# Other steps for the weight factors and the sums of blocks in the first attention

## The chip, the core and the metric

The kernel runs on one core of a Trainium2 chip. The metric is the time of the whole launch on the device, in microseconds, here the median of three runs. A core has a matrix engine (TensorE, in the profile PE, its weight loads PEld), an engine for elementwise work and reductions (VectorE, DVE), one for activation functions (ScalarE, ACT), GpSimd (POOL) and SyncE (SP), which in this kernel issues nearly all DMAs.

## What is computed

Two attention blocks, one after the other, on 8 images of 512 channels and 32 x 32 pixels (1024 tokens), all in float32. Each block normalises in 8 groups of channels, makes q, k and v, attends with 8 heads of 64 channels, projects and adds its input:

```python
def block(x, gamma, beta, wq, wk, wv, bq, bk, bv, wp, bp):     # for one image, x: (512, 1024)
    xg = x.reshape(8, -1)
    xn = (xg - xg.mean(-1)) * rsqrt(xg.var(-1) + 1e-5)
    xn = xn.reshape(512, 1024) * gamma + beta
    q, k, v = wq @ xn + bq, wk @ xn + bk, wv @ xn + bv         # 8 heads of 64 rows
    attn = softmax(q.T @ k / 8)                                # for each head, 1024 x 1024
    out = (attn @ v.T).T
    return x + wp @ out + bp

x = block(x, L0...)
x = block(x, L1...)
```

The two layers have weights of their own; in the reference they come as one stacked qkv matrix for layer 0 and as three matrices for layer 1.

## The kernel before

There are 16 jobs, an image and a layer each, in the order (image 0, layer 0), (1, 0), (0, 1), (1, 1), then the next two images. For each job the kernel runs an attention, and between two attentions a stretch of projections: v of the next job, the output projection of this job, then k and q of the next job. The projections use Strassen's scheme with seven products instead of eight (v one level deep, the others two levels), so weights and inputs are needed as sums of their blocks. That gives VectorE three kinds of work that the change and the prediction name:

- weight factors: four sums for each weight matrix (`factor`, L151 to L160; S1, S2, S3, S4), made once for each layer and matrix, written to DRAM by `store_factors` (L162, DMAs of L168) and read back later as tiles w of a ring of seven;
- sums of blocks of the normed input xn (`combine`, L380 to L391, tile t), and the deep sums of these (`inner_sums`, L401 to L429, tile deep);
- sums of blocks of the attention's output (L534 to L539, and `combine` on tile to), in the stretch after an attention.

`Attention.run` (L984) writes the attention down step by step. There are 8 groups (pair of heads, half of the queries) of 8 steps, 64 steps in all, numbered i. In a step TensorE makes the scores of step i (L870, tile sc) and the products with v of step i - 2 (L901, tile po); ScalarE takes the exponential (L875, tile e, from a pool of six); VectorE adds e to the sum of its group (L885 for a group's second step, L887 afterwards, tile acc). At a group's last product `finish` (L906) follows: VectorE reduces acc (L917, tile r) and adds the two halves of po into q (L924), which frees po's banks. Every second group a gather of r (L944) goes out by SP, later VectorE inverts the sums (`invert`, L948 to L968), SP spreads the inverses (rd, then rb, L961 and L963), and VectorE normalises q (L978). These follow at due times that the kernel's own count of microseconds sets (`later`, `advance`).

Other work is put into the steps as chores, one in a step. A taken step sends a chore on to the next free one:

```python
def put(i, fn):
    while i in chores:
        i += 1
    chores[i] = fn
```

In the attention of job n, chores prepare job n + 1. Only in the first attention (n = 0) are there, besides the weight factors of output layer 0 and v layer 1, also the statistics of the next image's norm. `norm_steps(1)` gives as its reads: four sums and four squares on ScalarE (L244, L252), between them `less_mean` (L249), and at the end `by_count` (L258, on VectorE, tile mv) with `gather` (L271): SP writes mv to DRAM as dm, in two DMAs (L275), and reads it back as gm (L279) when dm has landed. Its steps are `groups` (L286 to L291: VectorE on gm, then a power on GpSimd, then SP writes dg and reads it back as mr, L293 and L296), `factors` (L304 to L306, from mr) and four times `apply` (L311, xn on ScalarE). The factors of weights are put first, then the reads, then the steps with the sums of blocks, and the last four deep sums. The slot of each chore in the first attention, as `put` gives it out:

| chore | before | after |
|---|---|---|
| blocks of weights sent for | 2 | 2 |
| factors of output, layer 0; store | 12, 15, 18, 21; 22 | 8, 10, 12, 14; 15 |
| factors of v, layer 1; store | 24, 27, 30, 33; 34 | 16, 18, 20, 22; 23 |
| sums of the norm; less_mean | 4, 5, 6, 7; 8 | 4, 5, 6, 7; 9 |
| squares of the norm | 10, 11, 13, 14 | 11, 13, 17, 19 |
| by_count and gather | 16 | 21 |
| groups; factors of the norm | 23; 31 | 24; 30 |
| apply | 35, 36, 37, 38 | 34, 35, 36, 37 |
| sums of blocks | 41, 44, 47, 50 | 39, 41, 43, 45 |
| deep sums | 52, 54, 57, 59 | 47, 49, 51, 53 |

The order on TensorE, ScalarE and VectorE is the order in which the program is written, so a chore stands in VectorE's queue between two sums of e. SP's order follows from the program and from when its inputs are expected: in the first attention it is dm, dm, gm, r, store, rd, rb, rb, store, dg, mr before, and store, store, r, store, rd, dm, rb, rb, dm, store, gm, dg, mr after.

After the attention the banks of both halves of PSUM are given out anew (`banks`), and v's first products on the right half need po's last banks, which L924 frees.

Of the kernel before, what the change touches and what calls it, by code (L numbers as in the profile page):

```python
# [40 lines left out]
K, V, Q, O = range(4)  # L41
# [31 lines left out]
def fast_path(  # L73
# [34 lines left out]
    def later(delay, fn):  # L108
        todo.append((clock[0] + delay, fn))
# [36 lines left out]
    def load_blocks(w, layer, which):  # L146
        for i in range(2):
            for j in range(2):
                nc.sync.dma_start(w[:, 2 * j + i], raw_block(layer, which, i, j))

    def factor(w, part):  # L151

        if part == 0:
            nc.vector.tensor_add(w[:, S1], w[:, S3], w[:, A22])
        elif part == 1:
            nc.vector.tensor_sub(w[:, S2], w[:, S1], w[:, A11])  # L156
        elif part == 2:
            nc.vector.tensor_sub(w[:, S3], w[:, A11], w[:, S3])
        else:
            nc.vector.tensor_sub(w[:, S4], w[:, A12], w[:, S2])  # L160

    def store_factors(w, layer, which):  # L162
        keep = wdram.tile([P, NW, 2, CH], F32, name=f"keep_{which}_{layer}")
        if (which, layer) == (O, 1):
            nc.sync.dma_start(keep, w)
        else:
            for s in (slice(S1, NW), slice(S3, S3 + 1)):
                nc.sync.dma_start(keep[:, s], w[:, s])  # L168
        factors[which, layer] = keep
# [3 lines left out]
    def fetch():  # L173


        if not plan or len(held) == RING:
            return
        key = plan.popleft()
        n, which, o = key
        layer = jobs[n][1]  # L180
        w = ring.tile([P, NW, P], F32, tag="w", name=f"w_{which}_{n}_{o}")
        held[key] = w
        if (which, layer, o) in deep:
            nc.sync.dma_start(w, deep[which, layer, o])
        else:
            if o in BLOCK:
                src = raw_block(layer, which, *BLOCK[o])
            else:
                src = factors[which, layer][:, FACTOR[o]]
            nc.sync.dma_start(wide(w), src)  # L190
            if which != V:
                raw.add(key)
# [20 lines left out]
    def x_tile(b):  # L213
        xs[b] = xpool.tile([P, NC, S], F32, tag="x", name=f"x_{b}")
        return xs[b]

    def load_x(b):
        for cc in range(NC):
            nc.sync.dma_start(xs[b][:, cc, :], x[b, cc * P : (cc + 1) * P, :])

    class Norm:
# [20 lines left out]
        def sums(self, cc):  # L242

            nc.scalar.activation(  # L244
                xn[0][:, cc, :], xs[self.b][:, cc, :], AF.Identity, accum_out=self.mv[:, cc, 0:1]
            )
# [523 lines left out]
    def last_weights(n):  # L770
        w = acts.tile([P, NW, 2, CH], F32, tag="deep", name="w_last")
        nc.sync.dma_start(w, factors[O, jobs[n][1]])
        return w
# [10 lines left out]
    def last_sums(sh):  # L784


        def start():
            if sh == 0:
                tx[0] = acts.tile([P, 3, 2, HALF], F32, tag="t", name="t_last")
            nc.vector.tensor_sub(last_right(sh, 5), last_right(sh, 7), last_right(sh, 1))  # L790

        def second():
            nc.vector.tensor_sub(last_right(sh, 6), last_right(sh, 3), last_right(sh, 5))

        def third():
            nc.vector.tensor_sub(last_right(sh, 7), last_right(sh, 3), last_right(sh, 7))

        def fourth():
            nc.vector.tensor_sub(last_right(sh, 4), last_right(sh, 2), last_right(sh, 6))

        return start, second, third, fourth
# [241 lines left out]
    def deep_steps(n):  # L1043


        made = []

        def sums_(part, direct):
            if not made:
                made.append(True)  # L1050
                d = acts.tile([P, 4, 7, QT], F32, tag="deep", name=f"deep_{n}")
                deep_x[0], deep_t[0] = d[:, :, :4, :], d[:, :, 4:, :]
            inner_sums(part, direct)

        return [
            lambda part=part, direct=direct: sums_(part, direct)
            for direct in (True, False) for part in range(4)
        ]

    def extend_plan(n):  # L1060
        plan.extend((n, V, o) for o in ORDER)
        plan.extend((n - 1, O, o) for o in ORDER)
        plan.extend((n, which, o) for which in (K, Q) for o in OUTER)
# [29 lines left out]

        return load, [lambda oc=oc: add_up(oc) for oc in range(NC)]

    def first_factors(put, which_layers):

        box = []

        def start():  # L1100
            box.append(acts.tile([P, 2, NW, 2, CH], F32, tag="deep", name=f"raw_{len(factors)}"))
            for i, (which, layer) in enumerate(which_layers):
                load_blocks(box[0][:, i], layer, which)

        put(2, start)
        at = 9
        for i, (which, layer) in enumerate(which_layers):
            for part in range(4):
                at += 3
                put(at, lambda i=i, part=part: factor(box[0][:, i], part))  # L1110
            put(at + 1, lambda i=i, which=which, layer=layer: store_factors(
                box[0][:, i], layer, which
            ))
# [162 lines left out]
    for n in range(-1, len(jobs)):  # L1276
        last = n + 1 == len(jobs)
        outs = None
        if n >= 0:
            chores = {}  # L1280
# [6 lines that stand above are left out]
            if last:  # L1287
                w = last_weights(n)
                for i, fn in enumerate(last_sums(0)):
                    put(44 + 3 * i, fn)  # L1290
            else:
                if n == 0:
                    first_factors(put, [(O, 0), (V, 1)])
                elif n == 1:
                    first_factors(put, [(K, 1), (Q, 1)])
                elif n == 2:
                    first_factors(put, [(O, 1)])
                for i, (_, fn) in enumerate(extra):
                    put(2 + i, fn)
                at = (10, 19, 22, 24, 26, 28, 36, 39, 42, 45)  # L1300
                if n == 0:
                    for i, fn in zip((3, 3, 4, 5, 6, 8, 10, 11, 12, 13, 15), reads):
                        put(i, fn)
                    at = (22, 30, 34, 35, 37, 38, 41, 44, 47, 50)
                for i, fn in zip(at, steps + sums(n + 1)):
                    put(i, fn)
                deep_first = deep_steps(n + 1)
                for at, fn in zip((52, 54, 57, 59), deep_first[4:]):
                    put(at, fn)
                put(61, lambda: (extend_plan(n + 1), [fetch() for _ in range(RING)]))  # L1310
            assert max(chores, default=0) < NT * len(att.groups)
            att.run(chores)
            banks(0, "one")
            banks(1, "one")
            if last:
                for i, fn in enumerate(last_sums(1)):
                    later(7.0 + 0.8 * i, fn)
                later(13.0, judge)
                for sh in range(2):
                    last_proj(n, w, sh)  # L1320
                break
            outs = OutputSums(n)
            out_sums(n, outs)
            first = v_phase(n + 1, ORDER)
            for thunk in first[:-1]:
                thunk()
            rest = first[-1:]
            extra = deque()
            if jobs[n][1] == 1 and jobs[n][0] + 2 < B:
                extra.append((11, lambda b=jobs[n][0] + 2: (x_tile(b), load_x(b))))  # L1330
            if n == 1:
                load, bias_steps = make_out_bias(1)
                extra.append((8, load))
                extra.extend((11, fn) for fn in bias_steps)
            if n + 2 < len(jobs):
                reads, steps = norm_steps(n + 2)
                extra.extend((15, fn) for fn in reads)
        both = deep_phases(n + 1, extra, outs, deep_first[:4] if outs else ())
        both[0]()
        rest[0]()  # L1340
        if n < 0:
            later(22.0, lambda: load_x(1))
        for thunk in both[1:]:
            thunk()
        banks(0, "two")
        att = Attention(n + 1)
        att.scores(0)
        att.scores(1)
        banks(1, "two")
        att.scores(2, "po")  # L1350
# [249 lines left out]
```

## Time and profile before

| | us |
|---|---|
| median of three runs (lowest, highest) | 3205.2 (3205.03, 3205.63) |
| the profiled execution: time, span | 3206.06, 3204.3 |
| TensorE, VectorE, ScalarE busy | 3185.3, 2772.8, 1914.4 |
| first attention, TensorE from first scores to last product | 81.57 to 191.7 |
| stretch to the second attention | 191.7 to 287.13 |
| second attention; stretch to the third | 287.13 to 397.16; to 489.78 |

An attention takes 110 us, of which a step is 1.72; the stretch after the first attention takes 95.4 us, the one after the second 92.6. The span is what lies between the first and the last instruction; the execution's own time is 1.76 us longer. TensorE ran at its full clock throughout.

How it is to be read: in a timeline a line gives start and duration of an instruction (or of several alike, with xcount), its engine, its line in the kernel, what it writes and reads, and in brackets the time that the engine was idle before it and what ended that. In the chain of waits every piece is the one that the next had to wait for. An engine that is busy is not thereby the bound: what counts is whether TensorE waits for it.

### The profile page before, as it was taken

Reading aid. Unit: us, or ns where it says so; the run is one execution under the profiler, and the core shown is the slowest. Engines: PE = TensorE matmul, PEld = TensorE weight load, DVE = VectorE, ACT = ScalarE, POOL = GpSimd, SP = SyncE. Lnnn points to the kernel's source line nnn. Section 1 sums busy time; section 2 is a strip of 40 time slices with the busy share of each in tenths; the row PEclk is TensorE's granted clock in tenths of the full one; section 3 lists DMA queues with packets and bytes.
Section 4 is the critical chain, followed back from the end, with each engine's and each line's share of the span. In section 5 each row is a group of like instructions: output and inputs, shape, how many; then the busy total and the mean of one; then the engine's idle time right before and its main releaser. Section 6 shows DMA issues by size and latency. Waiting matters only on the chain.

```text
span 3204.3 us, 57789 instructions
## 1 busy us (share of the span) xinstructions
PE 3185.3 (99%) x22917; PEld 1862.8 (58%) x22917; DVE 2772.8 (87%) x3989; ACT 1914.4 (60%) x3063; POOL 100.7 (3%) x95
## 2 busy tenths in 40 slices
PE   9999999999999999999999999999999999999999
PEld 7366384563836638366483754837547375573744
DVE  8897999979889798897988879888898888978878
ACT  4746646466565665656656565565656656566564
POOL 0000000000000000000000000000000000000000
PEclk9999999999999999999999999999999999999999
DMA  8234172350613305034170421504316051150611
GB/s 291 74 107 127 48 213 70 92 169 22 210 28 88 91 26 159 22 100 132 33 211 16 114 72 33 152 16 135 103 44 194 16 137 48 49 136 16 174 37 42
DMA packets 156998, 308.32 MB, mean 96 GB/s; under 512 B 34104, under 2 KB 60592, under 8 KB 156464
## 3 DMA queue, kind: packets, MB, share of 16 engines
q1 hardware_dynamic: 139856, 272.05, 26.8%
q0 software_dynamic: 16864, 32.51, 6.2%
q8 instruction: 181, 2.97, 0.4%
q14 instruction: 97, 0.79, 0.1%
HBM read 225.13 MB, written 45.68 MB: 85 GB/s over the span
## 4 chain that ended last, share of the span: by engine, by line
PE 95%; DVE 3%; DMA 1%; issue 0%; POOL 0%; ACT 0%; DVEq 0%; ACTq 0%; POOLq 0%
PE sc L870 28%; PE po L901 27%; PE zd L636 10%; PE vd L636 10%; PE z L494 6%; PE yd L636 5%; PE ud L636 4%; PE v L494 2%; PE y L494 2%; PE u L494 1%; PE z_last L814 0%; DMA x<-p 0%; DVE w L156 0%; DMA w<-deep 0%; DVE p L655 0%; DVE v L520 0%
## 5 line engine op out<-in xcount | busy, mean ns | idle before, releaser
L875 ACT ACTIVATE e<-sc 128x1024 f32<-128x1024 f32 x1024 | 1045.3, 1025 | 563.4 <-PE sc L870 457.4
L870 PE MATMUL sc<-q,k 64*64 64x512 f32 x8192 | 1058.0, 589 | 0.0
L901 PE MATMUL po<-e,v 64*64 64x512 f32 x8192 | 1057.1, 589 | 0.0
L887 DVE TENSOR_TENSOR acc<-acc,e 128x1024 f32<-128x1024 f32 x768 | 936.0, 1219 | 58.8 <-ACT e L875 12.1
L901 PEld LDWEIGHTS po<-e,v 64*64 64x64 f32 x8192 | 312.9, 133 | 566.0 <-issue 554.4
L870 PEld LDWEIGHTS sc<-q,k 64*64 64x64 f32 x8192 | 311.2, 133 | 562.7 <-issue 545.0
L885 DVE TENSOR_TENSOR acc<-e,e 128x1024 f32<-128x1024 f32 x128 | 156.3, 1221 | 112.3 <-ACT e L875 112.2
L636 PE MATMUL zd<-deep,w 128*128 128x256 f32 x860 | 241.1, 380 | 3.8 <-DVE p L653 1.7
L636 PE MATMUL vd<-deep,w 128*128 128x256 f32 x804 | 224.3, 380 | 2.1 <-DVE p L655 1.3
L636 PEld LDWEIGHTS zd<-deep,w 128*128 128x128 f32 x860 | 162.8, 190 | 28.2 <-DVE p L653 3.0
L636 PEld LDWEIGHTS vd<-deep,w 128*128 128x128 f32 x804 | 152.3, 190 | 24.6 <-DVE p L655 2.5
L917 DVE TRANSPOSE_TENSOR_REDUCE r<-acc 128x32 f32<-128x1024 f32 x128 | 158.5, 1238 | 0.6
L682 POOL DMA_DIRECT2D x<-p x62 | 74.6, 1211 | 1972.7 <-ACT p L646 1525.2
L636 PE MATMUL vd<-os,w 128*128 128x256 f32 x420 | 118.1, 380 | 1.6 <-DVE p L655 1.5
L668 DVE TENSOR_TENSOR p<-p,p 128x1024 f32<-128x1024 f32 x94 | 114.2, 1214 | 0.0
L494 PE MATMUL z<-w,t 128*128 128x256 f32 x480 | 110.9, 379 | 0.0
L494 PE MATMUL z<-w,xn 128*128 128x256 f32 x480 | 110.1, 382 | 0.0
L518 ACT COPY v<-z 128x512 f32<-128x512 f32 x32 | 18.8, 586 | 148.7 <-PE z L494 148.7
L494 PEld LDWEIGHTS z<-w,xn 128*128 128x128 f32 x480 | 90.0, 190 | 23.8 <-issue 12.2
L442 ACT COPY ud<-zd 128x256 f32<-128x256 f32 x156 | 55.7, 357 | 76.6 <-PE zd L636 75.1
L653 DVE TENSOR_TENSOR p<-vd,s 128x256 f32<-128x256 f32 x63 | 26.7, 424 | 85.6 <-PE vd L636 85.6
L657 ACT COPY s<-vd 128x256 f32<-128x256 f32 x156 | 58.1, 373 | 69.2 <-PE vd L636 69.2
(242 smaller groups left out, 4194.9 us busy)
## 6 DMA issues: line engine op xcount, KB each, us to landing
w<-deep SPq DMA_DIRECT2D x287, 448.0 KB, 3.8
x<-p POOLq DMA_DIRECT2D x62, 512.0 KB, 6.9
rb<-rd SPq DMA_DIRECT2D x96, 256.0 KB, 4.0
w<-keep SPq DMA_DIRECT2D x84, 256.0 KB, 2.7
deep<-w SPq DMA_DIRECT2D x42, 448.0 KB, 3.8
w<-wqkv_dram SPq DMA_DIRECT2D x57, 256.0 KB, 2.8
x<-x_dram SPq DMA_DIRECT2D x28, 512.0 KB, 6.4
out_dram<-x SPq DMA_DIRECT2D x28, 512.0 KB, 6.2
```

Source lines behind the costliest of these rows:

```text
L442: nc.scalar.copy(u, z)
L494: nc.tensor.matmul(ps[:, ti * CH : (ti + 1) * CH], right(src, tx[0], o)[:, cc, t0 : t0 + P], w[:, cc, :], start=(start and ti == 0 and cc ...
L636: nc.tensor.matmul(ps, lhs[:, FACTOR[i], :], moving[i], start=start, stop=True, skip_group_check=True,)
L657: return chain(product, lambda ps: nc.scalar.copy(s5, ps), put, z, y, u, w)
L668: outer.append(lambda: nc.vector.tensor_add(to_, a, b))
L682: nc.gpsimd.dma_start(to_, p(part), accum_op=ALU.add)
L870: nc.tensor.matmul(sc[h * HD : (h + 1) * HD, j, :], k[r, hp, k0 : k0 + HD], q[r, hp, sh * HALF : (sh + 1) * HALF], start=True, stop=True,)
L875: nc.scalar.activation(e, sc, AF.Exp, scale=SCALE)
L885: nc.vector.tensor_add(acc[g], self.es[i - 1], e)
L887: nc.vector.tensor_add(acc[g], acc[g], e)
L901: nc.tensor.matmul(po[g][j * HD : (j + 1) * HD, h, :], v[r, kc, d0 : d0 + HD], e[r, j, :], start=(kc == 0), stop=(kc == NT - 1),)
L917: nc.vector.tensor_reduce(self.r[:, 0, m, :], self.acc.pop(g).rearrange("p j (b e) -> p (j b) e", e=RP), AX.X, ALU.add, apply_transpose=True,)
```

## The change

In the first attention the weight factors start at step 8 and stand in every second step, where they started at step 12 and stood in every third. The sums of blocks are put from step 39 in every second step, and the last four deep sums follow in every second step from 47. Nothing else of the program is edited; chores whose step is now taken move, as the table above shows. The same instructions run on TensorE, VectorE and ScalarE.

```diff
-    def first_factors(put, which_layers):
+    def first_factors(put, which_layers, at=9, apart=3):
 
         box = []
...
         put(2, start)
-        at = 9
         for i, (which, layer) in enumerate(which_layers):
             for part in range(4):
-                at += 3
+                at += apart
                 put(at, lambda i=i, part=part: factor(box[0][:, i], part))
             put(at + 1, lambda i=i, which=which, layer=layer: store_factors(
                 box[0][:, i], layer, which
             ))
...
                 if n == 0:
-                    first_factors(put, [(O, 0), (V, 1)])
+                    first_factors(put, [(O, 0), (V, 1)], 6, 2)
                 elif n == 1:
                     first_factors(put, [(K, 1), (Q, 1)])
...
                 if n == 0:
                     for i, fn in zip((3, 3, 4, 5, 6, 8, 10, 11, 12, 13, 15), reads):
                         put(i, fn)
-                    at = (22, 30, 34, 35, 37, 38, 41, 44, 47, 50)
+                    at = (22, 30, 34, 35, 36, 37, 39, 41, 43, 45)
                 for i, fn in zip(at, steps + sums(n + 1)):
                     put(i, fn)
                 deep_first = deep_steps(n + 1)
-                for at, fn in zip((52, 54, 57, 59), deep_first[4:]):
+                for at, fn in zip((47, 49, 51, 53) if n == 0 else (52, 54, 57, 59), deep_first[4:]):
                     put(at, fn)
```

## The prediction

> **What bounds the kernel now.** I read four views, each to find where the one before it ends: the chain of waits (what the end hangs on), the waits of TensorE (how much could be won at all), the timeline around the first attention (who is late there), and the DMA queue of SP (what the moved steps send for). The page's line for the chain of waits first:
>
> ```profile
> PE 95%; DVE 3%; DMA 1%; issue 0%; POOL 0%; ACT 0%; DVEq 0%; ACTq 0%; POOLq 0%
> ```
>
> TensorE is the bound; the other engines count only where TensorE waits for them. Its waits between 80 and 290 us, the stretch that the change can touch (columns: us in total, times, longest):
>
> ```profile
> PE zd L636 <- DVE p L653: 1.7, 2, 1.1
> PE v L494 <- DVE q L924: 1.7, 1, 1.7
> PE zd L636 <- ACT yd L438: 1.6, 1, 1.6
> PE vd L636 <- DVE p L655: 0.6, 1, 0.6
> ```
>
> Together 5.6 us. This is the ceiling of any gain: 5.6 of 3205.2 us is 0.17%. I call 0.2%, 6.4 us, the least that a measurement of this kernel tells from no change.
>
> The timeline shows why the 1.7 us wait is there. These are VectorE's instructions that matter, and TensorE's late one:
>
> ```profile
> 111.18 1.23 DVE L885 TENSOR_TENSOR acc<-e,e 128x1024 f32<-128x1024 f32 x1 [0.81 <-ACT e L875]
> 120.85 0.60 DVE L948 TENSOR_REDUCE lt<-r 32x64 f32<-32x256 f32 x1 [2.51 <-DMA r<-r]
> 126.71 0.21 DVE L286 BATCH_NORM_STATS2 gs<-gm 8x6 f32<-8x64 f32 x1
> 196.87 1.25 DVE L917 TRANSPOSE_TENSOR_REDUCE r<-acc 128x32 f32<-128x1024 f32 x1
> 198.03 0.65 DVE L924 TENSOR_TENSOR q<-po,px 128x512 f32<-128x512 f32 x1
> 198.74 1.99 PE L494 MATMUL v<-w,t 128*128 128x256 f32 x8 [1.67 <-DVE q L924]
> ```
>
> The bracket is the engine's idle time. VectorE idles 8.0 us in the first attention (0.40, 0.73, 0.72, 1.56, 0.26, 0.20, 0.82, 0.81 and 2.51), all before 120.85. After that it shows no bracket until 235: it is late and works off a queue. TensorE has done the attention at 191.7, VectorE at 198.7. From 194.3 to 230.05 the chain of waits is VectorE's, then TensorE's. So the quantity to follow is VectorE's idle time in the first attention: **its work is not changed in amount, so the end of its queue moves by the change in idle time, and TensorE with it.**
>
> The DMA queue of SP in that stretch:
>
> ```profile
> 110.43 1.36 SPq L275 DMA_DIRECT2D dm<-mv  x2
> 116.76 0.38 SPq L279 DMA_DIRECT2D gm<-dm  x1
> 117.24 2.28 SPq L944 DMA_DIRECT2D r<-r  x3
> 122.38 0.34 SPq L961 DMA_DIRECT2D rd<-rt  x1
> 124.94 1.30 SPq L963 DMA_DIRECT2D rb<-rd  x2
> 126.34 0.54 SPq L168 DMA_DIRECT2D keep<-raw  x1
> ```
>
> The gather of the norm (dm to DRAM, then gm back) starts at 110.43, right after VectorE scales mv (L258, 110.20). Gm is sent for at 116.76, after SP waited 4.9 us for dm. VectorE uses it at 126.71, unhindered. And r, which VectorE lacks at 118.3, was sent for only at 117.24 because it stood behind gm.
>
> [...] 9.95 us lie between gm's issue and its use, and gm waits 4.9 us for dm. [...] The trace: 3.8 us to landing for dm (2 KB, to DRAM), 1.7 for r (8 KB, within SBUF). [...]
>
> **The change part by part.**
>
> (1) *Eight weight factors* (L154 to L160, 0.68 us each, 0.60 from start to start), from steps 12 to 33 to steps 8 to 22. Before 112.3 us VectorE now runs five of them instead of two: 3 x 0.60 = 1.8 us more in time that it idled. Its idle there falls from 5.5 to 3.7 us. The blocks of weights that they read are sent for at 81.6 to 86.5 and land within 7.5 us, by 94; the first factor now stands at 95.8. Nothing is waited for. Gain 1.8 us. Stores of factors go to SP earlier, ahead of r; they wait for factors that are done by 108.4.
>
> (2) *What the factors push aside.* A step holds one chore; a taken step sends the chore to the next free one. The table of steps is filled with factors first, so the statistics of the next image move: the last square from step 14 to 19, and L258 with the gather from step 16 to 21. The first use of gm, groups (L286), was put at 22 and moves only from 23 to 24. **The distance between sending and using falls from 7 steps to 3, of 1.72 us each.** This is the cost of the change.
>
> I lay VectorE's new queue from L917 of group 1 on, which starts at 112.3 as before (it hangs on e of step 17). Start to start: L917 1.17, L924 0.57, sum 1.13, factor 0.60, two sums 2.46, factor 0.60, L948 to L968 1.67, sum 1.13: L258 at 121.6. Then 0.10, sum 1.13, factor 0.60, sum 1.13: VectorE is at groups at 124.6.
>
> On SP the gather now stands behind rd, and the two halves of dm are split: dm, rb, rb, dm, store of 768 KB, gm. The first dm goes at 121.7. Rb must wait for rd (120.2 plus 2.56, as 122.38 to 124.94): 122.7. Two rb of 0.65 each put the second dm at 124.0, the store at 124.7. From the second dm to gm the trace has 5.6 us here (111.18 to 116.76), and over the 15 gathers 4.9 on average, 3.8 to about 6. I take 4.9: gm is issued at 128.9. Its landing is not shown; it is bounded from above by attention 2, where gm is issued at 507.61 and used at 509.66 without idle time, so 2.05 us, and from below by r's 1.7. With 0.4 us for traffic: 131.3. **VectorE stands at groups for 131.3 - 124.6 = 6.7 us.** From both ends: 124.0 + 3.8 + 1.7 = 129.5, a stall of 4.9; and 124.0 + 6.0 + 2.05 + 2.2 for a ring full of rb and store = 134.2, a stall of 9.6. Queued behind are the sums of ACT's exponentials. With the stall they are some 9 us late; the pool has six buffers of e, so ACT waits for one or two of them, and then TensorE. I count about 3 us of TensorE in the attention. That is not added: TensorE has 1.67 us of waiting at the end anyway, plus what VectorE is later there.
>
> (3) *r before gm.* R no longer stands behind gm on SP. Sent for at 113.5, with 2.28 for three issues and 2.0, it is there by 117.8; VectorE comes to L948 at 118.7. The 2.51 us of idle time go. Gain 2.5 us.
>
> (4) *Sums of blocks and deep sums* (L385 to L391 at 1.13 us, L423 to L429 at 0.87), one to six steps sooner. VectorE is continuously busy there, so this only changes the order: no change in the sum. The normed input that they read is made by ACT from step 34 on; with the stall ACT gets its factors (L304 to L306) at about 143 instead of 141, is done by 151, and the first sum stands at 156. Cost nothing; if the stall were 5 us longer, this cover would be gone.
>
> Sum: 6.7 - 1.8 - 2.5 = **+2.4 us** at the end of VectorE's queue, and so at TensorE's restart (198.74 to 201.1). From there to 287.13 both engines do the same work in the same order, the DMAs that add into x start from products of TensorE, and the next 15 attentions hang on TensorE: the 2.4 us stay. The bounds of the stall give +0.6 and +5.3. The profiled execution took 3206.06 us, 1.76 over its span of 3204.3; it would take 3208.5, and the median goes from 3205.2 to **3207.6**.
>
> **Rivals.**
>
> *Gm is there in time* (the other side). It decides if gm lands before 128.9, where the stall is below the 4.3 us gained. For it: the fastest gathers of the trace need 4.45 us from the first dm to gm. Against it: rb stands between the two halves of dm. Without any stall VectorE would catch up with ACT and idle for e elsewhere, some 1.7 us by the same laying out, so at most 2.6 us are won: TensorE's 1.67 and the waits of 0.63 at 226 and at 230. 3202.6 us.
>
> *The traffic holds up the gather.* Two rb of 256 KB and a store of 768 KB share the rings with 2 KB of dm in pieces of 8 bytes. From a landing at 135.3 the loss passes 6.4 us; at 136.5 the stall is 11.9 and the loss 7.6: 3212.8 us. Against it: before, the same rb and store filled the DMA engines for only about 4 us.
>
> *Nothing shows.* Stall and gains meet within half a microsecond, or the lateness is worked off in the second half of the attention: 3205.2. Against it: no idle time is left there to work it off.
>
> **How the numbers follow.** Forecast 0.68, gm in time 0.14, traffic 0.08, nothing 0.10. The predicted time is the forecast's, 3207.6. The range reaches from 3204.5 to 3211.0, over the bounds of the stall and over "nothing"; outside are most of "gm in time" and "traffic". Faster by over 0.2% isn't in reach of any case, as TensorE has 5.6 us to give: 0.02 for what I have not seen, taken from "gm in time". Slower by over 0.2%: the traffic's 0.08 and 0.02 from the forecast's upper end, 0.10. Within: 0.88.
>
> **What would show it.** In the profile of the changed kernel: an idle bracket of 5 to 10 us before L286 with gm as its releaser; none before the first L948; SP with dm, rb, rb, dm and the store ahead of gm; TensorE with some waits for ACT about steps 32 to 40; TensorE's wait for L924 at about 201; the second attention starting at about 289.5 instead of 287.13. Wrong it is if gm's bracket is below 4 us, if VectorE idles after step 30, or if TensorE's restart and the second attention's start do not move alike.

## The result, and the profile after

| | before | after |
|---|---|---|
| median (lowest, highest), nine runs each, us | 3205.03 (3204.17, 3208.08) | 3214.11 (3212.74, 3216.72) |
| ratio of the times, with its 95% interval | | 1.0028 [1.0020, 1.0037] |
| the profiled execution: time, span, us | 3206.06, 3204.3 | 3214.24, 3212.4 |
| VectorE idle in the first attention, us | 8.01 | 15.93 |
| TensorE from the first scores to those of the second attention, us | 205.56 | 213.48 |

The changed kernel is 9.1 us slower, with an interval of 6.4 to 11.9. The profiled executions lie 8.2 us apart, and 7.92 of these are there when the second attention begins. The prediction had the direction and the place right and the size wrong: it had +2.4 us, and its range ended at 3211.0.

SyncE's queue in the timeline of the changed kernel, to be set beside the six lines of before (columns: start, duration, engine, line, what is written from what):

```profile
114.24 1.91 SPq L944 DMA_DIRECT2D r<-r  x3
121.03 0.33 SPq L961 DMA_DIRECT2D rd<-rt  x1
122.52 0.68 SPq L275 DMA_DIRECT2D dm<-mv  x1
123.30 1.88 SPq L963 DMA_DIRECT2D rb<-rd  x2
125.24 0.61 SPq L275 DMA_DIRECT2D dm<-mv  x1
125.94 0.55 SPq L168 DMA_DIRECT2D keep<-raw  x1
135.51 0.36 SPq L279 DMA_DIRECT2D gm<-dm  x1
```

R now goes out ahead of the gather, and the two halves of dm stand around rb, as laid out. But gm is sent for 10.3 us after the second dm. The timeline of VectorE in the same kernel, the instructions that frame this wait and the last one of the attention:

```profile
119.50 0.60 DVE L948 TENSOR_REDUCE lt<-r 32x64 f32<-32x256 f32 x1
124.22 1.22 DVE L887 TENSOR_TENSOR acc<-acc,e 128x1024 f32<-128x1024 f32 x1
137.51 0.22 DVE L286 BATCH_NORM_STATS2 gs<-gm 8x6 f32<-8x64 f32 x1 [12.07 <-DMA gm<-dm]
206.63 0.65 DVE L924 TENSOR_TENSOR q<-po,px 128x512 f32<-128x512 f32 x1
```

L948 no longer has the bracket of 2.51 us that it had: the wait for r is gone. In its place L286 waits 12.07 us for gm. After that VectorE shows no bracket until the end of the attention, so nothing of it is worked off; L924 is at 206.63 instead of 198.03. The chain of waits of the changed kernel gives the 12 us to the two transfers (columns: start, duration, what):

```profile
125.24 10.20 DMA dm<-mv
...
135.51 1.98 DMA gm<-dm
```

TensorE's waits between 80 and 300 us in the changed kernel (us in total, times, longest):

```profile
PE sc L870 <- ACT e L875: 5.1, 1, 5.1
PE zd L636 <- DVE p L653: 2.0, 2, 1.4
PE zd L636 <- ACT yd L438: 1.2, 1, 1.2
PE v L494 <- DVE q L924: 1.1, 1, 1.1
PE vd L636 <- DVE p L655: 0.6, 1, 0.6
```

The first line is new: with VectorE standing still, ScalarE has no free buffer for e (its line L875 waits 7.22 us for VectorE's L885), so it doesn't read the scores, and TensorE has no place for new ones. The wait for L924 is still there, so TensorE's restart follows the end of VectorE's queue, as before.

Why dm took so long is not a matter of bytes. The windows of one microsecond in the changed kernel, while rb and the second half of dm were queued (after the busy times come the granted clock, the busy share of the DMA engines and GB/s):

```profile
core 0: us, PE busy (x) PEld busy (x) DVE busy (x) ACT busy (x) POOL busy (x), PEclk, DMA share, GB/s
123.00:124.00 1.00, 1.00 (x16) 0.43 (x12) 1.00 (x2) 0.81 (x1) 0.00 (x0) 1.00 0.14 18
124.00:125.00 1.00, 1.00 (x14) 0.31 (x8) 1.00 (x2) 0.49 (x1) 0.00 (x0) 1.00 0.06 1
125.00:126.00 1.00, 1.00 (x16) 0.33 (x11) 0.45 (x1) 1.00 (x2) 0.00 (x0) 1.00 0.00 0
126.00:127.00 1.00, 1.00 (x16) 0.44 (x12) 0.00 (x0) 0.78 (x2) 0.00 (x0) 1.00 0.05 6
127.00:128.00 1.00, 1.00 (x15) 0.31 (x8) 0.00 (x0) 0.31 (x2) 0.00 (x0) 1.00 0.15 29
128.00:129.00 1.00, 1.00 (x15) 0.32 (x11) 0.00 (x0) 0.96 (x1) 0.00 (x0) 1.00 0.11 27
129.00:130.00 1.00, 1.00 (x16) 0.44 (x12) 0.00 (x0) 0.34 (x1) 0.00 (x0) 1.00 1.00 301
```

Rb was issued from 123.30 on, and the DMA engines stay nearly idle until 129 (a share of 0.15 at most). Only then does it move in earnest, at 301 GB/s. Its landing took 7.7 us, against 3.8 before. The two dm are 2 KB each.

The trace also counts the packets, the single transfers that a DMA is made of, and tells them apart by size: a piece of dm is one of 8 bytes, rb's are of 2 KB. Here are the first half of dm, the gap behind it, and the start of rb, as the counts of the changed kernel have them for the stretches 123.30 to 124.94, 124.94 to 126.97 and 126.97 to 129.00:

```profile
DMA packets 273, 0.02 MB, mean 11 GB/s; under 512 B 272, under 2 KB 272, under 8 KB 272
DMA packets 0, 0.00 MB, mean 0 GB/s; under 512 B 0, under 2 KB 0, under 8 KB 0
DMA packets 30, 0.06 MB, mean 30 GB/s; under 512 B 0, under 2 KB 0, under 8 KB 30
```

So writing the small pieces is quickly done: those of the first half are out by 124.94. (The 272 are its 256 pieces and 16 more small packets, as in before, where the two halves have 544; the large one is counted in an instruction queue.) Then nothing moves for 2.0 us, rb trickles for 2.0 more, and at 129 it flows. In before, rb is issued at 124.94 and flows from 126.52, 1.6 us later. The pieces of the second half of dm come between 130.23 and 131.37, when 205 packets of rb's 256 are out, and gm is sent for 4.1 us after the last of them. In before those 4 us are there too: the last piece of dm is out by 112.71, gm is sent for at 116.76, and no packet moves in between. From the second dm's issue to its last piece, however, it is 6.1 us for 1.5. That is where the extra time lies: ahead of its last piece, not behind it.

### The profile page after: what moved, and what is told of

Read it like the earlier page. It is cut to its first block, busy times and chain, and to the rows that moved or that the text cites. A ratio compares the mean times of both kernels' runs of the same rounds, so it can differ in the third digit from the quotient of the medians.

```text
span 3212.4 us, 57788 instructions
## 1 busy us (share of the span) xinstructions
PE 3188.0 (99%) x22917; PEld 1863.2 (58%) x22917; DVE 2773.1 (86%) x3989; ACT 1914.4 (60%) x3063; POOL 99.7 (3%) x95
## 4 chain that ended last, share of the span: by engine, by line
PE 93%; DVE 5%; DMA 1%; issue 1%; ACT 0%; SPq 0%; DVEq 0%; POOL 0%; ACTq 0%; POOLq 0%
PE sc L870 26%; PE po L901 26%; PE zd L636 10%; PE vd L636 10%; PE z L494 6%; PE yd L636 5%; PE ud L636 4%; PE v L494 2%; PE y L494 2%; PE u L494 1%; DVE acc L887 1%; PE z_last L814 0%; DMA x<-p 0%; DMA dm<-mv 0%; DVE w L156 0%
## 5 line engine op out<-in xcount | busy, mean ns | idle before, releaser
L875 ACT ACTIVATE e<-sc 128x1024 f32<-128x1024 f32 x1024 | 1044.7, 1024 | 571.3 <-PE sc L870 456.7
L885 DVE TENSOR_TENSOR acc<-e,e 128x1024 f32<-128x1024 f32 x128 | 156.4, 1222 | 111.1 <-ACT e L875 111.0
```

The lines of the kernel that those rows point to most:

```text
L875: nc.scalar.activation(e, sc, AF.Exp, scale=SCALE)
L885: nc.vector.tensor_add(acc[g], self.es[i - 1], e)
```

## The experiments

Theory 1, after the result: the whole loss is the longer wait for gm, and it comes from rb standing between the halves of dm. Theory 2: the sums of blocks, moved up to six steps, cost something of their own. Theory 3, which came in later: three steps between the gather and its use are too few wherever the gather stands. Of two more, the expectations of e5 to e7 call it the ring theory that dm is late because it stands behind rb in SyncE's queue (its ring), and the load theory that dm is slow whenever rb and the store move.

All runs in one table. The rule of the prediction is tested along with them: "rest" is the time from the start of L885, the attention's first sum, to the start of its last L924, less VectorE's idle time in between, and should be the same in every kernel if only idle time counts. The column "to second attention" is TensorE's time from the first scores to those of the second attention. All times are in us.

| kernel | VectorE idle | rest | to second attention | median us (before beside it) | ratio [95%] |
|---|---|---|---|---|---|
| before | 8.01 | 104.80 | 205.56 | 3205.03 | |
| after | 15.93 | 104.84 | 213.48 | 3214.11 (3205.03) | 1.0028 [1.0020, 1.0037] |
| e1_sums_only | 7.27 | 104.80 | 204.70 | 3204.89 (3205.12) | 0.9999 [0.9991, 1.0008] |
| e2_factors_only | 15.39 | 104.93 | 212.38 | 3212.43 (3205.12) | 1.0024 [1.0014, 1.0033] |
| e3_reads_first | 5.60 | 104.90 | 202.55 | 3203.70 (3205.12) | 0.9996 [0.9988, 1.0004] |
| e4_groups_later | 9.09 | 104.94 | 206.79 | 3207.20 (3205.12) | 1.0007 [1.0001, 1.0014] |
| e5_dm_pool | 10.49 | 104.81 | 207.81 | 3208.38 (3205.09) | 1.0009 [1.0001, 1.0018] |
| e6_gather_apart | 6.66 | 105.16 | 204.45 | 3204.47 (3205.09) | 0.9997 [0.9989, 1.0005] |
| e7_gather_late | 8.20 | 104.72 | 206.85 | 3206.52 (3205.09) | 1.0004 [0.9995, 1.0012] |
| e8_dm_rows | 9.41 | 104.79 | 206.29 | 3207.07 (3204.44) | 1.0009 [1.0000, 1.0017] |
| e9_one_step | 5.60 | 104.70 | 202.58 | 3203.01 (3204.44) | 0.9996 [0.9987, 1.0004] |

**Either part alone.** E1 keeps the new steps of the sums and gives the factors their old ones; e2 is the opposite.

```diff
# e1_sums_only, against after
-                    first_factors(put, [(O, 0), (V, 1)], 6, 2)
+                    first_factors(put, [(O, 0), (V, 1)])
# e2_factors_only, against after
-                    at = (22, 30, 34, 35, 36, 37, 39, 41, 43, 45)
+                    at = (22, 30, 34, 35, 37, 38, 41, 44, 47, 50)
...
-                for at, fn in zip((47, 49, 51, 53) if n == 0 else (52, 54, 57, 59), deep_first[4:]):
+                for at, fn in zip((52, 54, 57, 59), deep_first[4:]):
```

> The sums of blocks and the deep sums at the changed steps (from 39 and from 47), the weight factors at the steps of before (12 to 33), so the gather of the norm stays at step 16. If the loss is the stall for gm (theory 1), nothing of it is here: 3204 to 3206 us, no idle time before L286. If the sums, standing closer together, crowd out the sums of e (theory 2), most of the 9 us are here: 3210 us or more.

> The weight factors at the changed steps (8 to 22), the sums of blocks and the deep sums at the steps of before (from 41 and from 52). Theory 1: the whole loss is here, 3212 to 3216 us, with 10 to 13 us of idle time before L286. Theory 2: 3207 us or less.

E1 took what before takes and e2 nearly what after takes, with 11.28 us of bracket at L286 and rb landing in 7.5 us. Theory 2 falls as the cause of the loss. The loss is in the factors' steps.

**The same factors, with the gather left early.** E3 puts the reads of the norm first and the factors around them, so the gather stands at step 15 and its use at 24; the factors then stand at 9, 14, 16, 17 and 19 to 22.

```diff
# e3_reads_first, against after
+                    for i, fn in zip((3, 3, 4, 5, 6, 8, 10, 11, 12, 13, 15), reads):
+                        put(i, fn)
                     first_factors(put, [(O, 0), (V, 1)], 6, 2)
...
-                    for i, fn in zip((3, 3, 4, 5, 6, 8, 10, 11, 12, 13, 15), reads):
-                        put(i, fn)
```

> All of the change, but the statistics of the norm are given their steps before the weight factors, so that by_count and the gather stand at step 15 and groups still at 24. Theory 1: no stall at L286; what the change gains is left (1.8 us of earlier factors, part of the 2.5 us of r), 3202 to 3204 us, and TensorE's wait for L924 is gone. Theory 2: still 3210 us or more.

The bracket at L286 is gone, L948 waits 0.70 us, and TensorE no longer waits for L924. So the early factors do no harm: what they push aside does. The median is 1.4 us below that of before, and the interval reaches from a gain of 1.2 thousandths to a loss of 0.4: not told apart from before.

**The use later.** E4 leaves the gather where after has it and puts groups and what follows up to nine steps later.

```diff
# e4_groups_later, against after
-                    at = (22, 30, 34, 35, 36, 37, 39, 41, 43, 45)
+                    at = (33, 39, 41, 42, 43, 44, 46, 48, 50, 52)
...
-                for at, fn in zip((47, 49, 51, 53) if n == 0 else (52, 54, 57, 59), deep_first[4:]):
+                for at, fn in zip((54, 56, 58, 60) if n == 0 else (52, 54, 57, 59), deep_first[4:]):
```

> All of the change, the gather at step 21 as there, but groups put at 33 instead of 22, the norm's factors at 39, apply from 41, the sums of blocks at 46, 48, 50, 52 and the deep sums at 54, 56, 58, 60. VectorE comes to L286 after 138, when gm has landed (137.5). Theory 1: no stall, the gain of 1.8 and 2.5 us is left as far as VectorE has no new idle time: 3202 to 3204 us. Theory 2, or if the late apply and sums cost: 3206 us or more.

That missed. Groups didn't wait any more, but the timeline of VectorE in this kernel has another wait:

```profile
132.27 1.23 DVE L978 TENSOR_TENSOR q<-q,rb 128x1024 f32<-128x1024 f32 x1 [4.69 <-DMA rb<-rd]
```

Rb itself is late. The gather's order harms two users, and the second had been hidden behind the first: in after VectorE comes to L978 only at 141. The theory had to be widened: not only does gm wait for rb, rb waits for something too.

**The gather apart from rb.** E6 is e4 with the gather four steps later, so that rb goes out before both halves of dm.

```diff
# e6_gather_apart, against e4_groups_later
-                    for i, fn in zip((3, 3, 4, 5, 6, 8, 10, 11, 12, 13, 15), reads):
+                    for i, fn in zip((3, 3, 4, 5, 6, 8, 10, 11, 12, 13, 25), reads):
```

> As e4, with the gather at step 25 instead of 21, so that rb and the store of 768 KB are issued before the first dm. Ring theory: rb lands in about 4 us, as before the change, not in 7.7; from the first dm to gm it is 4.5 to 6.5 us again, as VectorE's L258 comes some us after rb has flowed. Load theory or a slow gather in this place of the program: 9 us or more. The time is that of e4 if gm is in time at step 33.

Rb, issued at 120.51, moves at 207 GB/s between 122 and 123, and L978 doesn't wait. From the first dm to gm it is 4.16 us, where after has 13.0. Both are quick once they don't meet. The expectation had the time of e4; it came out 2.7 us lower, as the wait of L978 is gone too.

**The distance alone.** E7 is the kernel before with only the gather moved to step 20, with its use at 23.

```diff
# e7_gather_late, against before
-                    for i, fn in zip((3, 3, 4, 5, 6, 8, 10, 11, 12, 13, 15), reads):
+                    for i, fn in zip((3, 3, 4, 5, 6, 8, 10, 11, 12, 13, 20), reads):
```

> The kernel before with one edit: by_count and the gather at step 20 instead of 16, groups at 23 as before. The distance is 3 steps as in the change, but both halves of dm go out one after the other and gm before rb. Ring theory: from the first dm to gm 4.5 to 6.5 us, a stall at L286 of 1 to 4 us, and r no longer stands behind gm (2.5 us gained): 3204 to 3207 us. If the short distance alone makes the loss: a stall of 8 us or more and 3210 us or more.

With as few steps of distance as in after, L286 waits 2.17 us instead of 12.07, and r isn't waited for. The order on SyncE is dm, dm, rd, gm, rb. Equal steps are not equal times: from the first dm to VectorE's arrival at L286 it is 5.8 us here and 2.9 in after. These 2.9 us more are distance; the other 7.0 of the 9.9 us of stall saved are the gather's own time, 7.9 us from the first dm to gm's use for 15.0. Theory 3 falls as the main cause.

**One step.** E9 is after with L258 and its gather put at step 20 ahead of the factors, of which one moves from 20 to 21. The gather then stands one step sooner than in after, and ahead of VectorE's inversion.

```diff
# e9_one_step, against after
+                    put(20, reads[-1])
                     first_factors(put, [(O, 0), (V, 1)], 6, 2)
...
-                    for i, fn in zip((3, 3, 4, 5, 6, 8, 10, 11, 12, 13, 15), reads):
+                    for i, fn in zip((3, 3, 4, 5, 6, 8, 10, 11, 12, 13), reads[:-1]):
```

> All of the change, but by_count and the gather have step 20 and the factors that stood at 20 and 22 follow at 21 and 22; groups stay at 24. One step earlier L258 comes before VectorE's inversion, so both halves of dm go out before rd and rb, and gm before rb. If what is behind what on SP makes the loss and not the distance in steps, dm to gm is 4.5 to 6.5 us, the stall at L286 1 to 3.5 us, below the 4.3 us gained: 3202.5 to 3205 us. If the distance makes it, the stall is 8 us or more and the time over 3209 us.

The timeline of SyncE in this kernel:

```profile
119.09 1.34 SPq L275 DMA_DIRECT2D dm<-mv  x2
120.52 0.55 SPq L961 DMA_DIRECT2D rd<-rt  x1
123.46 0.35 SPq L279 DMA_DIRECT2D gm<-dm  x1
123.90 1.27 SPq L963 DMA_DIRECT2D rb<-rd  x2
```

and that of VectorE:

```profile
126.65 0.22 DVE L286 BATCH_NORM_STATS2 gs<-gm 8x6 f32<-8x64 f32 x1 [1.38 <-DMA gm<-dm]
```

The halves of dm follow each other and gm is sent for 4.37 us after the first. Rb, issued at 123.90 when dm has landed, moves at 277 GB/s between 126 and 127. One step takes 10.3 us off VectorE's idle time and 10.9 off the way to the second attention. Of the 10.7 us that go from the stall at L286, 3.3 are more time between its sending and its use, and 7.4 are the gather's own time, 7.6 us from the first dm to gm's use for 15.0. The median is 1.4 us below that of before, where that of after is 9.1 above it. Against before it is as e3: a little lower, and not told apart.

**Whether it is SyncE's own queue.** E5 sends the two dm from GpSimd's queue instead.

```diff
# e5_dm_pool, against after
-                nc.sync.dma_start(
+                (nc.gpsimd if self.n == 1 else nc.sync).dma_start(
```

> All of the change, but the two DMAs that write dm in the first attention go out from GpSimd's queue instead of SP's. If the second half of dm is late because it stands in SP's rings behind rb (ring theory), dm is now down about 5 us after L258, rb lands in about 4 us again, gm is issued by 128.5 and the stall is 3 to 6 us: 3204 to 3208 us. If dm is slow whenever rb and the store move (load theory), gm stays at 134 or later: 3211 us or more.

About half came back: L286 waits 6.64 us. Gm is sent for at 128.77, but takes 3.4 us to land. Of the DMA engines the share is 0.56 between 124 and 125, as one rb moves, then at most 0.12 from 126 to 130, and the other rb flows only from 130 on. Stall and time are just above what was expected, and the part that stayed is the point: a dm in another queue still goes with idle engines and a late rb. So the order within SyncE's queue isn't all of it. The edit changes more than the queue, though: in GpSimd's queue both halves of dm together are 64 packets, where before has 544 for them.

One time may be alike in e5 and in after. In after the last packet of the first half of dm is out at 124.94, and rb flows 4.1 us later. In e5 something moves up to about 126 (the share is 0.35 between 125 and 126 and 0.00 between 126 and 127), though the windows don't say whether the last of it is dm, and the late rb flows from 130. That suggests that rb, which reads from DRAM, waits for the end of dm's writes to DRAM; it isn't shown. In e9 rd, itself a write to DRAM issued just behind dm, is out by 122 (10 GB/s between 121 and 122, none from 122 to 124), before gm is sent for at 123.46. No run tests the suggestion.

**The pieces.** A half of dm is 256 pieces of 8 bytes in DRAM. E8 lays dm out by partition, so that a half is 64 pieces of 32 bytes; gm is then read by two DMAs, one for each half. Below L285 its line numbers are 10 higher.

```diff
# e8_dm_rows, against after, for the first attention's gather alone
...
+                dm = dram.tile([2, HD, NC, 2], F32, tag="dm", name=f"dm_{self.n}")
+                for h in range(2):
+                    nc.sync.dma_start(dm[h], self.mv[h * HD : (h + 1) * HD])
...
+                for h in range(2):
+                    nc.sync.dma_start(
+                        self.gm[h * NC : (h + 1) * NC], dm[h].rearrange("p c k -> c p k")
+                    )
```

> All of the change, but in the first attention dm is laid in DRAM as mv lies in SBUF, so that a half of dm is 64 pieces of 32 bytes instead of 256 of 8; gm is read back in two DMAs with pieces of 8 bytes, the second behind the store of 768 KB. If the small pieces are why a half of dm takes long and holds up rb, rb lands in about 4 us and dm in 2 to 3, the first gm is issued by 130, and VectorE's stall is 5 to 9 us (its end then hangs on the second gm): 3206 to 3211 us. If it is the latency of a write to DRAM whatever its pieces, rb still lands late (7 us or more) and gm goes at 134 or later: 3213 us or more.

The timeline of SyncE in this kernel, with dm and rb in the same order as in after:

```profile
121.64 0.49 SPq L276 DMA_DIRECT2D dm<-mv  x1
122.23 1.92 SPq L973 DMA_DIRECT2D rb<-rd  x2
124.20 0.60 SPq L276 DMA_DIRECT2D dm<-mv  x1
124.89 0.49 SPq L279 DMA_DIRECT2D gm<-dm  x1
...
127.71 0.25 SPq L279 DMA_DIRECT2D gm<-dm  x1
```

The first half has landed by 124.89, 3.25 us after its issue, and the second 3.5 us after its own. And the windows of the same kernel, at the time when the engines of after were idle:

```profile
124.00:125.00 1.00, 1.00 (x12) 0.31 (x8) 0.56 (x1) 1.00 (x2) 0.00 (x0) 1.00 0.54 201
125.00:126.00 1.00, 1.00 (x16) 0.34 (x12) 0.00 (x0) 0.78 (x2) 0.00 (x0) 1.00 0.72 212
126.00:127.00 1.00, 1.00 (x16) 0.42 (x12) 0.00 (x0) 0.37 (x1) 0.00 (x0) 1.00 0.89 292
```

Rb moves before 124 (57 GB/s between 123 and 124), less than 1.8 us after its issue at 122.23, and lands in 4.5 us instead of 7.7. The bracket at groups falls from 12.07 to 5.54 us. So it is the layout of dm, 256 pieces of 8 bytes for each half, that holds rb up in this order of issue. The edit changes the number of pieces, their size and their places in DRAM at once, and no run takes these apart. The 5.54 that stay are dm and gm in turn, close before their use.

## Why the prediction was wrong

**The step that failed** is part (2), and in it one term: "from the second dm to gm ... I take 4.9", with bounds of 3.8 to about 6. It was 10.27 us. All else in the stall came out: SyncE's order, dm, rb, rb, dm and the store; VectorE at groups at 125.44, which is 124.8 counted from the start of before's attention (after's starts 0.65 later), where 124.6 stood; the second dm at 124.6 so counted, for 124.0; gm's way 2.0 us for 2.4. The sum of these differences, 5.4 + 0.6 - 0.4 - 0.2, is the 5.4 us between the stall of 12.07 and "VectorE stands at groups for 6.7 us".

Why the term was wrong: it was taken from 15 gathers, whose halves go out back to back with no rb of 256 KB between them. (The largest of the 15 is 6.78 us, at 297 us, not "about 6"; that would still have bounded the stall at about 10.) The prediction saw that rb stands there and added 0.4 us of traffic, or 2.2 at the worst, estimates that it doesn't derive. It counted rb and the store as bytes that have to pass. The cost was another: rb hardly moved for 5.7 us, from its issue to 129, while the engines were idle, and the second half of dm was behind it. Of the 10.27 us, 6.1 passed before the last piece of that half was written, and 4.1 after it. Whether the store, which moves in these 4.1 us, has a part in them is open, since no run takes it alone away; before has as much without it.

**The rival that came out** is "the traffic holds up the gather", given 0.08: a stall of 11.9, a loss of 7.6 and 3212.8 us stand there, and 12.07, 7.92 and 3214.1 were measured. Its numbers held, and that was luck: 136.5 for gm's landing was not derived from a duration. Its mechanism held only in part: it named the pieces of 8 bytes and the queue they share with rb, and meant a queue full of bytes. What spoke against it, that the same rb and store had filled the DMA engines for only about 4 us, was true (a mean share of 0.82 between 126 and 131) and no evidence, because in before no dm with small pieces was under way just ahead of rb. A term whose every sample lacks the thing that is new has no bounds from these samples; the chance of 0.08 was too low for that.

What in the DMA engines held rb stays open. The end of dm is long: in before no packet moves in the 4.05 us between dm's last piece and the issue of gm, and in after gm is sent for 4.1 us after dm's last piece. But that explains little of the loss, since it is there in both kernels; and in e5 dm has landed by 128.77, while most of the second rb is still to come. Order in the queue is open too: in after 205 of rb's 256 packets are out before the pieces of the second dm, but no run isolates why. E8 ties the late rb to how dm is laid out in DRAM (4.5 us to its landing for 7.7), e5 shows that another queue does not free it (the second rb flows from 130), and the 4.1 us of after between dm's last packet and rb's flow are a hint, not a proof.

**What held.**

- The rule "the end of its queue moves by the change in idle time, and TensorE with it". The rest is 104.70 to 105.16 us in all eleven kernels, over idle times from 5.60 to 15.93. TensorE's way less this idle time is less even, 196.88 to 198.65, so idle time alone gives it to about 2 us. From before to after the idle time grew by 7.92 us and the way to the second attention by 7.92.
- Parts (1) and (3), a gain of 1.8 and 2.5, together 4.3: outside the stall the idle time fell from 8.01 to 3.86, by 4.15. The wait for r went (2.51), and that for e fell from 5.50 to 3.86.
- Part (4) at nothing: e1. Its warning, that with a stall 5 us longer the cover of the first sum would be gone, didn't come true: the stall was 5.4 longer, the normed input was done at 156.7, and the sum stands at 162.46 with no bracket, because VectorE is as late as ScalarE.
- TensorE's waits in the attention, "about 3 us" and not added: one of 5.1 us, and not added was right, since TensorE still waits 1.1 us for L924.
- The ceiling of 5.6 us for any gain: the two best orders, e3 and e9, show 1.4 us each.

## What to carry to other kernels

When a list of slots sends a displaced entry on to the next free one, look first at what the displaced entries send for, and in which order the DMA queue then has them: here a gather that moved five steps lost 8 us net, and one step back gave it all back. A transfer small in bytes need not be small in time: here 2 KB in 256 pieces went out just ahead of 256 KB that were needed soon, and rb landed in 7.7 us where it had taken 3.8, while from the first dm to gm it was 13.0 us for 6.3. In such a case try another order, or a layout in larger pieces. And where a new order puts two transfers side by side that no row shows together, the durations of either alone bound nothing from above.

## What the runs showed of the hardware beyond this

In the changed kernel TensorE's gap of 5.1 us cost more than the gap. The timeline of TensorE, around it:

```profile
134.56 1.04 PE L901 MATMUL po<-e,v 64*64 64x512 f32 x8
140.70 1.98 PE L870 MATMUL sc<-q,k 64*64 64x512 f32 x8 [5.10 <-ACT e L875]
142.46 1.93 PE L901 MATMUL po<-e,v 64*64 64x512 f32 x8
144.16 1.40 PE L870 MATMUL sc<-q,k 64*64 64x512 f32 x8
```

The same group of eight takes 1.04 us ahead of the gap and 1.9 to 2.0 after it. The windows of the same kernel have the granted clock for it (the column before the DMA share):

```profile
140.70:142.40 1.70, 1.70 (x8) 0.55 (x12) 1.70 (x3) 0.86 (x1) 0.00 (x0) 0.50 0.00 0
142.40:144.10 1.70, 1.70 (x12) 0.49 (x8) 1.60 (x2) 0.48 (x1) 0.00 (x0) 0.50 0.08 12
144.10:145.40 1.30, 1.30 (x13) 0.39 (x9) 1.20 (x2) 0.54 (x1) 0.00 (x0) 0.69 0.00 0
145.40:147.00 1.60, 1.60 (x20) 0.57 (x16) 1.50 (x2) 1.36 (x2) 0.00 (x0) 1.00 0.00 0
```

The granted clock is 0.50 for about 4 us after the gap, then 1.00. E2, with a gap of 4.3 us, shows the same: 0.50 between 138 and 142, and groups of 1.99 and 1.93 us. In e4 and e5, with gaps of at most 1.6 us in the attention, the clock stays at 1.00 there; in before the longest wait of TensorE is 1.7 us, and the mean clock 1.000. So in these runs the clock was halved with gaps of 4.3 and 5.1 us and not with gaps of 1.7 us and less; what lies between wasn't run. The prediction hadn't counted it. Here it lay beside VectorE's lateness and cost nothing that can be seen; TensorE's busy time is 3188.0 us for 3185.3. Where TensorE has no later wait to take it up, such a gap would cost about 2 us more, an estimate from these groups: the three after the gap take 4.70 us from start to start, and the three ahead of 134.56, at a clock of 1.00, take 2.57.
